# Unpacking the gate and up weights of the last feed-forward earlier, by way of a buffer in memory

## The chip, the core and the metric

The kernel runs on one core of a Trainium2 chip. The metric is the device time of one execution in microseconds (us). The engines of the core are TensorE (PE in the profile; its weight loads are PEld), VectorE (DVE), ScalarE (ACT), GpSimd (POOL) and SyncE (SP), which here only issues transfers (DMA). Each engine takes its instructions in a fixed order, and an instruction that waits holds up all that stand behind it on the same engine.

## What is computed

A decoder of two layers on 4 sequences of 512 tokens with 512 features. Each of the six steps is followed by a residual sum and a layer norm:

```python
x = _layernorm(x + _L0_attn_ref(x, ...))     # A: attention with rotary positions
x = _layernorm(x + _L0_xattn_ref(x, ...))    # B: cross attention
x = _layernorm(x + _L0_ffn_ref(x, ...))      # C: ternary weights, 8-bit activations, Hadamard
x = _layernorm(x + _L1_attn_ref(x, ...))     # D: causal attention, 16 heads
x = _layernorm(x + _L1_xattn_ref(x, ...))    # E: cross attention with a mask
x = _layernorm(x + _L1_ffn_ref(x, ...))      # F: weights packed in 4 bits
```

The change is about the weights of F. Its reference, cut down:

```python
def _dequant_fp4(packed_i32, scales_f16, group_size):
    nib = w[:, :, None] >> shifts & jnp.uint32(15)      # eight 4-bit codes in a word
    vals = _FP4_LUT[nib.astype(jnp.int32)].reshape(out_f, in_p * 8)
    return vals * s_full                                # one scale for each group of 128
w_gu = _dequant_fp4(gate_up_packed, gate_up_scales, GROUP_SIZE)
w_down = _dequant_fp4(down_packed, down_scales, GROUP_SIZE)
gate_up = jnp.einsum('bsh,oh->bso', x, w_gu)
gate, up = (gate_up[..., :I], gate_up[..., I:])         # I = 1408
h = jax.nn.silu(gate) * up
y = jnp.einsum('bsi,hi->bsh', h, w_down)
return y / jnp.sqrt(jnp.mean(y * y, axis=-1, keepdims=True) + 1e-6)
```

## The kernel before

The letters A to F above name the six steps in the kernel too, with the number of the sequence: F0 is the last feed-forward on sequence 0. `lanes` runs two of these at a time. Each is a Python generator; it records instructions up to a `yield`, then the other goes on. So the end of one step is recorded among the beginning of the next: the last of C beside D0, E3 beside F0. A `Pipe` defers a piece of work by some yields. From what is recorded a scheduler makes each engine's order, in which an instruction may stand well before or behind the place where it was recorded.

Weights are prepared by further generators, kept in `net.bg`. The list `BESIDE` says during which steps such a generator is advanced by one yield at each round; `need` runs one on until the weights that a step is about to use are there.

All tiles are 128 partitions wide and 2 KB deep. They come from pools of fixed numbers of buffers: `o` (69 buffers: weights, operands and probabilities), `t` (13, short-lived), `x` (12, rows of the residual) and `w` (4, raw weights as they are loaded). A tile can be filled when the last reader of the buffer's former tile is done. Nearly all loads and stores go through SP's one queue, in order.

F's gate and up weights are 22 tiles of 128 x 512: 11 slices of 128 hidden features, each with a gate tile (u = 0) and an up tile (u = 1); the down weights are 11 tiles. In memory a packed word stands eight times, once for each of its codes, so that a packed tile has the size of the unpacked one, 256 KB. `l1_ffn_weights` unpacks on VectorE. For gate and up there are three instructions a tile: the shifts (L1024), the mask (L1025) and the multiplication by 2^126 (L1030) that makes the code's bits a number; the scale is put on behind the matmul (`scaled`, L1064, L1067, L1070). For down weights the first two are the same, the third puts the scale on as well (L1034), and the tile is split into a high part (ScalarE, L139) and a low one (GpSimd, L142). The packed tile is loaded to a `w` buffer, worked on in place, and only the third step writes an `o` tile, `gu`. This generator, "F", is advanced beside E2, and otherwise by `need` at the head of each slice in F0. F1 to F3 find all weights unpacked.

In `l1_ffn` each slice takes 16 matmuls (L1106), one for each of the 4 groups of features, the high and the low part of x, and gate and up; then the scales, SiLU (L1078), the product (L1082), its split (L1087, L1088), and 12 matmuls for the down weights (L1097).

The end of C matters too: its 16 Hadamard results are stored to a scratch in memory (L638), loaded again in another layout (`z`), go through matmuls (L715), a maximum on VectorE (L661), a copy (L663), five small operations, a scaling on ScalarE (L681), a rounding on VectorE (L682), transposes and the down projection (L701).

Of the kernel before, what the change touches and what calls it, by code (L numbers as in the profile page):

```python
# [10 lines left out]
F32 = mybir.dt.float32  # L11
F32R = mybir.dt.float32r
F16 = mybir.dt.float16
BF16 = mybir.dt.bfloat16
I32 = mybir.dt.int32
U8 = mybir.dt.uint8
AF = mybir.ActivationFunctionType
ALU = mybir.AluOpType
# [3 lines left out]
B, S, D = 4, 512, 512  # L22
P = 128
# [9 lines left out]
D_NEXT = 7  # L33
B_NEXT = 13
F_LOAD = 5
F_SCALED, F_ACT, F_PAIR, F_DOWN = 1, 5, 3, 9
ORDER = "A0 A1 A2 A3 B0 B1 B2 B3 C0 C1 C2 C3 D0 D1 D2 D3 E0 E1 E2 E3 F0 F1 F2 F3"

BESIDE = [("A1", "A3", "C0"), ("A3", "B0", ("B", 0)), ("B0", "B2", "C"), ("C3", "D0", "D"), ("E2", "E2", "F")]


class Pipe:


    def __init__(self):
        self.todo = []
# [21 lines left out]
class Net:  # L68
    def __init__(self, ctx, tc, args):
        self.tc = tc  # L70
        self.nc = tc.nc
        self.a = args
        self.n = 0
        pool = lambda name, **kw: ctx.enter_context(tc.tile_pool(name=name, **kw))
        self.const = pool("const", bufs=1)
        self.op = pool("op", bufs=O_BUFS)
        self.tp = pool("tp", bufs=T_BUFS)
        self.xp = pool("xp", bufs=X_BUFS)
        self.wp_ = pool("wp", bufs=W_BUFS)
        self.small = pool("small", bufs=4)  # L80
        self.psum = pool("psum", bufs=8, space=PSUM)
        nc = self.nc
        tc.keep_in_program_order(nc.scalar.preload_act_table_set(LOG_EXP))
        self.ident = self.c("ident", [P, P])
        make_identity(nc, self.ident)
        self.ident16 = self.c("ident16", [P, P], BF16)
        nc.vector.tensor_copy(self.ident16, self.ident)
        self.ones = self.c("ones", [P, P])
        nc.gpsimd.memset(self.ones, 1.0)
        scratch = lambda name, shape: nc.dram_tensor(name, shape, F32, kind="Internal").ap()  # L90
        self.had_scratch = scratch("had_scratch", (2, NT, 2048, P))
        self.xd = [args["x"]] + [scratch(f"x{i}", (B, S, D)) for i in range(1, 6)] + [args["out"]]
        self.bg, self.table = {}, None
        self.gu, self.dn = {}, []
        self.pre = {}
        self.w1 = {}
        self.mean, self.scale = {}, {}
        self.tern = {name: {} for name in self.TERNARY}
# [909 lines left out]
        yield from self.value_rows(pipe, pT, cn, x, em[:, 8:12], 4, b)  # L1008


    def l1_ffn_weights(self):

        nc, a = self.nc, self.a
        pipe = Pipe()
        i4 = self.load(self.c("i4", [P, 3], I32), a["i4"])
        sh4, msk4, c6 = i4[:, 0:1], i4[:, 1:2], i4[:, 2:3]
        gs = self.load(self.c("gs16", [P, 88], F16), a["gu_s"])
        self.gs = self.c("gs", [P, 88])
        with self.tc.issue_after(self.mark.ins):
            nc.vector.tensor_copy(self.gs, gs)  # L1020

        def bits(w):

            nc.vector.tensor_scalar(w, w, sh4, c6, ALU.logical_shift_left, ALU.arith_shift_right)  # L1024
            nc.vector.tensor_scalar(w, w, msk4, None, ALU.bitwise_and)  # L1025
            return w.bitcast(F32)

        def codes(i, u, w):
            self.gu[i, u] = self.o("gu", F32R)
            nc.vector.tensor_scalar(self.gu[i, u], bits(w), 2.0 ** 126, None, ALU.mult)  # L1030

        def down(w, sc):
            f = bits(w)
            nc.vector.scalar_tensor_tensor(f, f, 2.0 ** 126, sc, ALU.mult, ALU.mult)  # L1034
            self.dn.append(self.split(f, "p4", lo_eng=nc.gpsimd))

        for i in range(11):
            for u in range(2):
                pipe.tick()
                pipe.later(F_LOAD, codes, i, u, self.load(self.w("p4", I32), a["gu_p"][i, u]))  # L1040
                yield
            pipe.tick()
            sc = self.load(self.t("p4s", F16), a["dn_s"][i : i + 1, :].to_broadcast([P, 512]))
            pipe.later(F_LOAD, down, self.load(self.w("p4", I32), a["dn_p"][i]), sc)
            yield
        yield from pipe.drain()
# [90 lines left out]
def lanes(order, task, step):  # L1137

    todo = [(e.strip("+!"), e[0] == "+", max(1, e.count("!"))) for e in order]
    plain = [name for name, _, _ in todo]
    live, done = {}, set()
    n, said = 0, 9
    while todo or live:
        if todo and len(live) < 2:
            name, soon, times = todo[0]
            before = chr(ord(name[0]) - 1) + name[1]
            if (before in done or before not in plain) and (said >= times or not live or soon):
                todo.pop(0)  # L1150
                live[name] = task(name)
                last = name
                n, said = n + 1, 0
        for name, g in list(live.items()):
            word = next(g, "end")
            if word == "end":
                live.pop(name)
                done.add(name)
            elif word == "next" and name == last:
                said += 1  # L1160
        step(n)


def body(tc, args, phases=range(6)):
    with ExitStack() as ctx:
        net = Net(ctx, tc, args)
        net.gamma = net.load(net.c("gamma", [P, 1]), args["gamma"].to_broadcast([P, 1]))
        if 0 in phases:
            net.l0_attn_weights()
        net.bg = {("B", 0): net.l0_xattn_ctx(0), "C0": net.l0_ffn_scales(), "C": net.l0_ffn_weights(), "D": net.l1_attn_weights(), "F": net.l1_ffn_weights()}  # L1170
        f = [net.l0_attn, net.l0_xattn, net.l0_ffn, net.l1_attn, net.l1_xattn, net.l1_ffn]
        plain = ORDER.replace("+", "").replace("!", "").split()
        order = ORDER.split() if len(phases) == 6 else ["ABCDEF"[p] + str(b) for p in phases for b in range(B)]

        def step(n):
            if len(phases) == 6:
                for first, last, key in BESIDE:
                    if plain.index(first) < n <= plain.index(last) + 1:
                        next(net.bg[key], None)

        def start(name):
            return f["ABCDEF".index(name[0])](int(name[1]))

        lanes(order, start, step)
# [68 lines left out]
```

## Time and profile before

| | us |
|---|---|
| median of 3 runs | 1629.89 |
| lowest and highest of them | 1626.9, 1636.79 |
| the profiled execution | 1630.29 |
| its span, from the first to the last instruction | 1628.6 |
| DMA issued by SP that carry packed gate and up words (22 of 256 KB), from issue to landing | 2.7 |

In the profile a stretch of time is given in us from the span's start. A row of busy time by stretch has the stretch, its length, then for each engine the busy time and in brackets the number of instructions, and at the end PE's granted clock, the share of the transfer engines and GB/s. A row of one line's instructions has the least, the median and the greatest duration in ns. A row of the timeline has the start, the duration, the engine, the line, the operation and the tiles (written <- read). By these rows, C3 ends near 780 us, D runs from 760 to 1160, E from 1150 to 1280, F0 from 1264 to about 1390, and F1 to F3 take 80 us each.

### The profile page before, as it was taken

To read this page: it belongs to the slowest core of one execution; us is meant where nothing else is said; L and a number is where in the kernel's file an instruction comes from. 1 tells how busy PE (TensorE), PEld (TensorE's weight loads), DVE (VectorE), ACT (ScalarE), POOL (GpSimd) and SP (SyncE) were. 2 spreads that over 40 slices of the span, in tenths; PEclk is the share of its full clock that TensorE was granted. 3 is DMA by queue.
4 is the path that set the end of the run, shared out by engine and by line. 5 is a ranking of instruction groups with operands and counts; after the bars stand their busy time and mean duration, and the time that the engine had idled before them with its cause. 6 is when DMAs were issued, how large, how long until landed. Compare 5 with 4: busy or idle time off the path is not lost.

```text
span 1628.6 us, 25543 instructions
## 1 busy us (share of the span) xinstructions
PE 1532.3 (94%) x8215; PEld 1100.0 (68%) x8246; DVE 1247.6 (77%) x2684; ACT 1010.6 (62%) x2177; POOL 665.9 (41%) x672
## 2 busy tenths in 40 slices
PE   7999999999999999899999999999998889999995
PEld 5888786444544664476777767777676766687774
DVE  6476589999875788977575766657779898979795
ACT  4333336988777887787796756967543445454542
POOL 6663563555535204422334243342333244333332
PEclk9999999999999999999999999999999999999998
DMA  7143344455124734861523334232446331111000
GB/s 241 35 149 123 110 149 137 146 172 174 59 75 132 222 116 136 250 188 61 145 60 77 79 90 117 60 86 68 155 155 196 128 113 53 43 37 52 1 26 26
DMA packets 127812, 180.76 MB, mean 111 GB/s; under 512 B 16560, under 2 KB 51376, under 8 KB 127680
## 3 DMA queue, kind: packets, MB, share of 16 engines
q1 hardware_dynamic: 123552, 170.69, 33.7%
q0 software_dynamic: 4128, 8.46, 2.1%
q8 instruction: 65, 1.06, 0.3%
q14 instruction: 67, 0.55, 0.1%
HBM read 111.98 MB, written 41.94 MB: 95 GB/s over the span
## 4 chain that ended last, share of the span: by engine, by line
PE 61%; DVE 17%; ACT 9%; issue 5%; DMA 4%; POOL 3%; SPq 1%; DVEq 0%; ACTq 0%; POOLq 0%
PE fg L1106 7%; PE facc L1097 6%; PE dT L883 3%; PE bo L458 2%; ACT de L873 2%; PE dn L701 2%; PE bT L213 2%; DVE x L200 2%; PE pu L649 2%; PE bs L486 2%; DVE bsm L434 2%; PE pg L647 2%; PE do L903 2%; DVE fg L1070 2%; PE dq L150 2%
## 5 line engine op out<-in xcount | busy, mean ns | idle before, releaser
L1070 DVE SCALAR_TENSOR_TENSOR fg<-fg,gs,fg 128x512 f32<-128x512 f32 x220 | 162.4, 745 | 35.4 <-PE fg L1106 15.2
L869 DVE CUSTOM_DVE_ANT_0 de<-ds,negm,thr 128x128 f32<-128x128 f32 (+3 forms) x256 | 126.4, 546 | 34.3 <-PE ds L858 31.2
L1106 PE MATMUL fg<-fxh,gu 128*128 128x512 f32 x352 | 143.7, 408 | 8.0 <-DVE fg L1070 5.0
L873 ACT ACTIVATE de<-de,dm 128x128 f32<-128x128 f32 (+3 forms) x256 | 143.1, 563 | 12.4 <-DVE dm L869 11.9
L1106 PE MATMUL fg<-fxl,gu 128*128 128x512 f32 x352 | 138.8, 394 | 0.0
L442 POOL TENSOR_SCALAR be<-be,bsm 128x512 f32<-128x512 f32 x128 | 95.8, 761 | 104.5 <-DVE bsm L440 72.8
L624 POOL TENSOR_TENSOR hl<-g,hh 128x512 fp32r<-128x512 f32 x64 | 83.9, 1318 | 113.3 <-ACT hh L623 98.7
L1074 POOL TENSOR_TENSOR fg<-fg,fg 128x512 f32<-128x512 f32 x44 | 61.1, 1388 | 127.1 <-ACT fg L1067 74.5
L436 ACT ACTIVATE be<-bs,bsm 128x512 f32<-128x512 f32 x128 | 87.3, 690 | 31.3 <-DVE bsm L434 29.6
L800 POOL TENSOR_TENSOR dql<-dqf,dqh 128x512 fp32r<-128x512 f32 x32 | 41.3, 1290 | 155.3 <-ACT dqh L799 121.0
L883 PE MATMUL dT<-ident,de 128*128 128x128 f32 x640 | 89.6, 278 | 7.6 <-ACT de L873 5.8
L1106 PEld LDWEIGHTS fg<-fxh,gu 128*128 128x128 f32 x352 | 66.9, 190 | 38.4 <-DVE fg L1070 14.8
L883 PEld LDWEIGHTS dT<-ident,de 128*128 128x128 f32 x640 | 71.7, 141 | 25.3 <-ACT de L873 13.6
L1064 ACT ACTIVATE fg<-fg,gs 128x512 f32<-128x512 f32 x88 | 60.4, 686 | 39.2 <-PE fg L1106 38.6
L434 DVE TENSOR_REDUCE bsm<-bs 128x1 f32<-128x512 f32 x128 | 83.3, 672 | 0.0
L1097 PE MATMUL facc<-p4h,fhh 128*128 128x512 f32 x176 | 71.2, 406 | 8.9 <-DVE fg L1070 6.2
L458 PE MATMUL bo<-bpT,cT 128*64 128x512 f32 x256 | 76.9, 618 | 2.1 <-ACT bpT L449 1.2
L213 PEld LDWEIGHTS bT<-ident,be 128*128 128x128 f32 x512 | 55.0, 141 | 34.6 <-issue 10.3
L213 PE MATMUL bT<-ident,be 128*128 128x128 f32 x512 | 73.2, 281 | 4.4 <-POOL be L442 2.1
L1067 ACT ACTIVATE fg<-fg,gs 128x512 f32<-128x512 f32 x44 | 30.3, 688 | 73.4 <-PE fg L1106 73.4
L312 POOL TENSOR_TENSOR z<-z,rope_cos 128x512 f32<-128x512 f32 x32 | 45.7, 1438 | 73.0 <-DVE zs L310 66.0
L1106 PEld LDWEIGHTS fg<-fxl,gu 128*128 128x128 f32 x352 | 66.8, 190 | 11.9
(332 smaller groups left out, 4693.3 us busy)
## 6 DMA issues: line engine op xcount, KB each, us to landing
x<-x SPq DMA_DIRECT2D x176, 256.0 KB, 3.1
had_scratch<-hw SPq DMA_DIRECT2D x64, 256.0 KB, 2.4
z<-had_scratch SPq DMA_DIRECT2D x64, 256.0 KB, 5.8
stk<-dqh SPq DMA_DIRECT2D x192, 64.0 KB, 2.0
tw<-in_wg_t SPq DMA_DIRECT2D x32, 256.0 KB, 3.8
tw<-in_wu_t SPq DMA_DIRECT2D x32, 256.0 KB, 3.6
tw<-in_wd_t SPq DMA_DIRECT2D x32, 256.0 KB, 2.9
p<-in_gu_p SPq DMA_DIRECT2D x22, 256.0 KB, 2.7
```

The costliest lines, as they stand in the source:

```text
L213: self.nc.tensor.transpose(pt[:, i * P : (i + 1) * P], srcs[i][:, j * P : (j + 1) * P], self.ident)
L434: nc.vector.tensor_reduce(sm[:, h : h + 1], ps, AX.X, ALU.max, negate=True)
L436: nc.scalar.activation(e, ps, AF.Exp, bias=sm[:, h : h + 1], accum_out=sm[:, 2 + h : 3 + h])
L442: nc.gpsimd.tensor_scalar(es[h][i], es[h][i], sm[:, 4 + h : 5 + h], 1.0, ALU.mult, ALU.mult)
L458: nc.tensor.matmul(po[0][h * 64 : h * 64 + 64, :], cT[j][:, c : c + 64], pTs[h], start=j == 0, stop=j == NT - 1)
L624: nc.gpsimd.tensor_tensor(lo, g, hi.bitcast(F32), ALU.subtract)
L869: nc.vector.tensor_tensor_reduce(es[i], ps, self.negm[:, 384 - P * i :], -1.0, self.thr[:, i : i + 1], ALU.add, ALU.min, n4[:, i : i + 1])
L873: nc.scalar.activation(es[i], es[i], AF.Exp, bias=n4[:, i : i + 1], scale=-1.0, accum_out=den[:, hh * 4 + i : hh * 4 + i + 1])
L883: nc.tensor.transpose(pt[:, o + (i - j) * P : o + (i - j + 1) * P], es[i][:, j * P : (j + 1) * P], self.ident)
L1070: nc.vector.scalar_tensor_tensor(y[u], ps, s, y[u], ALU.mult, ALU.add)
L1097: nc.tensor.matmul(acc[t], h[l][:, c], self.dn[i][r], start=i == 0 and n == 0, stop=i == 10 and n == 2)
L1106: nc.tensor.matmul(ps, self.gu[i, u][:, g * P : (g + 1) * P], xT[g][n], start=n == 0, stop=n == 1)
```

## The change

A new generator "F0" (`l1_ffn_codes`) takes over the unpacking of the gate and up tiles. It is advanced beside D1 to D3, three yields for each tile. It unpacks each to a `w` buffer and, two yields later, stores that to a new buffer in memory, `gu_codes`. `l1_ffn_weights` now loads each gate or up tile from there straight to its `o` buffer; the down weights are unpacked as before. The constants for the shifts and the mask are loaded by the new generator. (The diff's line numbers beyond L40 move by 2, and those of `l1_ffn` by 18.)

```diff
+CODES_EVERY = 3
...
-BESIDE = [("A1", "A3", "C0"), ("A3", "B0", ("B", 0)), ("B0", "B2", "C"), ("C3", "D0", "D"), ("E2", "E2", "F")]
+BESIDE = [("A1", "A3", "C0"), ("A3", "B0", ("B", 0)), ("B0", "B2", "C"), ("C3", "D0", "D"), ("D1", "D3", "F0"), ("E2", "E2", "F")]
...
+        self.gu_codes = scratch("gu_codes", (22, P, 512))
...
-    def l1_ffn_weights(self):
+    def l1_ffn_codes(self):
...
-        def codes(i, u, w):
-            self.gu[i, u] = self.o("gu", F32R)
-            nc.vector.tensor_scalar(self.gu[i, u], bits(w), 2.0 ** 126, None, ALU.mult)
+        self.bits = bits
+
+        def codes(n, w):
+            v = self.w("gu")
+            nc.vector.tensor_scalar(v, bits(w), 2.0 ** 126, None, ALU.mult)
+            pipe.later(2, lambda: nc.sync.dma_start(self.gu_codes[n], v))
+
+        for n in range(22):
+            pipe.tick()
+            pipe.later(2, codes, n, self.load(self.w("p4", I32), a["gu_p"][n // 2, n % 2]))
+            for _ in range(CODES_EVERY):
+                yield
+        yield from pipe.drain()
+
+    def l1_ffn_weights(self):
+
+        nc, a, bits = self.nc, self.a, self.bits
+        pipe = Pipe()
...
-                pipe.later(F_LOAD, codes, i, u, self.load(self.w("p4", I32), a["gu_p"][i, u]))
+                self.gu[i, u] = self.o("gu", F32R)
+                self.load(self.gu[i, u].bitcast(F32), self.gu_codes[i * 2 + u])
                 yield
...
-        net.bg = {..., "F": net.l1_ffn_weights()}
+        net.bg = {..., "F0": net.l1_ffn_codes(), "F": net.l1_ffn_weights()}
```

More of the change, by code (lines that the diff above doesn't have):

```diff
@@ L1169, in body @@
             net.l0_attn_weights()
-        net.bg = {("B", 0): net.l0_xattn_ctx(0), "C0": net.l0_ffn_scales(), "C": net.l0_ffn_weights(), "D": net.l1_attn_weights(), "F": net.l1_ffn_weights()}
+        net.bg = {("B", 0): net.l0_xattn_ctx(0), "C0": net.l0_ffn_scales(), "C": net.l0_ffn_weights(), "D": net.l1_attn_weights(), "F0": net.l1_ffn_codes(), "F": net.l1_ffn_weights()}
         f = [net.l0_attn, net.l0_xattn, net.l0_ffn, net.l1_attn, net.l1_xattn, net.l1_ffn]
```

## The prediction

> **What bounds the kernel now.** I read the page first, then the busy time by stretch, then the rows of the unpacking lines, the waits and the chain. The page says that no engine is full over the whole span:
>
> ```profile
> span 1628.6 us, 25543 instructions
> PE 1532.3 (94%) x8215; PEld 1100.0 (68%) x8246; DVE 1247.6 (77%) x2684; ACT 1010.6 (62%) x2177; POOL 665.9 (41%) x672
> ```
>
> So the stretch matters. The stretches from where the work is taken (1220 to 1380 us: the last cross attention and the first batch F0 of the last feed-forward), where it goes (690 to 780 us), and two to compare with, columns PE, PEld, DVE, ACT, POOL busy:
>
> ```profile
> 690.00:780.00 90.00, 87.54 (x608) 64.12 (x617) 68.28 (x178) 68.87 (x112) 22.63 (x29) 1.00 0.43 131
> 1160.00:1200.00 40.00, 40.00 (x198) 32.97 (x198) 33.99 (x68) 14.80 (x34) 10.72 (x10) 1.00 0.39 131
> 1220.00:1280.00 60.00, 51.54 (x247) 41.79 (x245) 55.89 (x114) 22.28 (x49) 21.61 (x17) 0.97 0.55 180
> 1280.00:1380.00 100.00, 92.36 (x382) 67.25 (x381) 94.82 (x161) 47.48 (x78) 42.16 (x30) 1.00 0.30 91
> 1380.00:1460.00 80.00, 76.57 (x337) 60.60 (x337) 67.26 (x113) 39.78 (x69) 29.37 (x22) 1.00 0.12 40
> 1460.00:1540.00 80.00, 76.91 (x332) 60.93 (x331) 65.53 (x111) 39.64 (x69) 30.66 (x23) 0.98 0.08 27
> 1500.00:1520.00 20.00, 20.00 (x89) 16.54 (x89) 15.60 (x22) 9.29 (x15) 8.07 (x7) 1.00 0.23 79
> ```
>
> DVE is nearly full from 1220 to 1380 (150.7 of 160 us). PE's busy time looks high, but its count of matmuls doesn't: 382 in 100 us beside F0, 669 in the 160 us of the next two batches, 89 in 20 us where nothing waits. From 690 to 780 DVE has 21.7 us idle, and PE is at 87.5 of 90. The unpacking itself:
>
> ```profile
> L1024 DVE TENSOR_SCALAR p<-p,i x33: 507/539/1607, 670.2 to 1359.4; 128x512 int32<-128x512 int32 x33
> L1025 DVE TENSOR_SCALAR p<-p,i x33: 450/476/1483, 675.8 to 1360.2; 128x512 int32<-128x512 int32 x33
> L1030 DVE TENSOR_SCALAR gu<-p x22: 392/416/1517, 1220.3 to 1359.9; 128x512 fp32r<-128x512 f32 x22
> 1330.24 1.48 DVE L1024 TENSOR_SCALAR p<-p,i 128x512 int32<-128x512 int32 x1
> 1331.64 0.41 DVE L1030 TENSOR_SCALAR gu<-p 128x512 fp32r<-128x512 f32 x1
> 1331.98 0.47 DVE L1025 TENSOR_SCALAR p<-p,i 128x512 int32<-128x512 int32 x1
> 1332.38 0.53 DVE L1024 TENSOR_SCALAR p<-p,i 128x512 int32<-128x512 int32 x1
> ```
>
> From start to start the three steps take 0.46, 0.40 and 0.34 us, 1.20 a tile; where POOL is working one of them can last 1.5 us.
>
> **Taken out beside F0.** 1280 to 1380 holds L1024 14.59 us, L1025 9.41 and L1030 5.39. Two thirds of the first two belong to gate and up, so DVE loses 16.0 + 5.4 = 21.4 of 94.8 us, which leaves 73.4. At the next batches' share of DVE (67.26 of 80) that needs 87.4 us. PE's 382 matmuls need 91.4 us at the next batches' pace and 85.8 us at the dense one. The gain is 8.6 to 14.2; I take 10.5, as DVE's own figure (12.6) lies between. PE is late next: in the built program its order beside F0 turns into the even pattern of the later batches.
>
> **Taken out of the cross attention.** 1220 to 1280: (7.91 + 6.01) x 2/3 + 6.17 = 15.5 us of DVE out of 55.9. At the pace of 1160 to 1200 (198 in 40 us) the 247 matmuls would need 49.9 us, so at most 10 us come free, at least none: the chain there also has a context load of 4.03 us (1224.05) and POOL's L142, which stay. I take 3.5.
>
> **Loads instead of packed words.** 22 loads take the place of 22, of the same 256 KB, 2.8 us to landing. They now wait for a buffer of the large pool on SP's queue, where before DVE's last step did. Behind the first five stand the context loads of batch 2, behind the next ten the context loads of batch 3, stores and F0's x. The tiles that held these buffers are read last by matmuls and copies of batches 0 to 2, the latest of the first fifteen by transposes of batch 1's probabilities near 1242; the store behind them went out at 1248.5. Nothing to 3 us; I take 0. The four word buffers now hold only down weights, so four L1034 and their splits move up to 1172 (three more there, 0.6 us each, in 6 idle us of DVE before 1200): 0 to 1.8, taken as 0.
>
> **Put in at 690 to 780.** The order of the built program tells what the diff doesn't: nearly all tiles are unpacked ahead of or just behind the first projections of the causal attention, within the end of layer 0's feed-forward, from the rows of 669 us on; only two tiles' steps stand near 800. 62 of the 66 instructions stand before 775. Eight such already ran there (four tiles' first two steps, for one of them down weights), so 54 are new: x 0.40 = 21.6 us into 21.7 idle ones. That idle time is mostly waiting in a chain (7.7 us for ACT's L681, 7.0 for the down projection), and every maximum, scale and rounding of that chain stands behind an inserted step. If half of it can be used, DVE slips by some 10 us; PE's matmuls follow in a fixed order, but the last steps lie behind the last split that PE needs (766). I take 7, with 0 (all of it fits; a gain has no source) and 21.6 (nothing fits) as ends.
>
> The stores wait on SP for the last step of a tile. Ahead of the 16 z loads of the last batch, which went out at 718.5, now stand the stores of the seventh and eighth tile, whose steps fall at about 715 and 720: SP's queue passes DVE's slip on to z, and so to L715. A store there takes 0.85 us of the transfers (256 KB at the 307 GB/s of 720 to 730). That is part of the 7. Later stores stand ahead of x stores and loads for batches not begun, which cost nothing, and of the first stk copies at 770, 4 us behind their own step.
>
> **Put in at 795 to 830.** Eight steps for down weights and four for gate and up, 0.43 us each: 5.2 us, where ACT is busy 19.4 of 20 us (800 to 820) and fed by DVE, which has 6.6 idle us there. I take 1, ends 0 and 5.2.
>
> **POOL's part.** Of the 33 rows of L1024, the 14 that overlap work on POOL last 1.18 us on average, the other 19 last 0.53; POOL works 36% of 1220 to 1280 and 42% of 1280 to 1380, but 0.3 us in the 10 from 710. So a step is dear where it is taken and cheap where it is put, and both sums above have it, as they use each place's rows. The Trainium skill, "SBUF — State Buffer", section "Who interferes with whom", has the reason: such an operation and GpSimd share a pair of ports, and the second to come is blocked for the whole instruction; the trace agrees. Were all steps priced at their usual 0.53, 0.47 and 0.41 us, DVE would lose 10.7 x 1.00 + 13 x 0.41 = 16.0 us beside F0 and not 21.4, need 93.7 us there, and the gain would be 6.3.
>
> **Sum.** The profiled execution took 1630.29 us, 0.4 above the median. 1630.3 - 10.5 - 3.5 + 7 + 1 = 1624.3. This is the likeliest case (chance 0.50, itself 1617 to 1631).
>
> **Rivals.** *Nothing comes of it* (0.26): other waits follow. Beside F0 the chain also passes POOL (L142 1.67 us at 1353.68, L1074 1.43 at 1356.60), and PE's waits are for ACT as much as for DVE (L1064 2.4 us against L1070 1.6). Against it, DVE is at 20.0 of 20 from 1320 to 1360. The gain would be the 8.6 alone, against 8: 1630. By the Trainium skill, "Perfetto Trace Analysis", section "Identifying the Most-Contended Engine", occupancy tells the bound for VectorE; over the whole span DVE is at 77%, and work that stays on DVE would then change nothing. The trace speaks for going by stretch.
>
> *All of it comes back* (0.14): both full stretches shrink to the dense pace and the insertion finds its holes: 14.2 + 10 - 3 = 21 less, 1609. For it: the batches after F0 run with idle DVE. Against it: the waits at the borders of batches (PE 8.72 of 10 at 720; 16.37 of 20 at 1200, with DVE at 10) have other causes.
>
> *The end of layer 0's feed-forward becomes DVE's* (0.10): DVE would need 68.3 + 21.6 = 89.9 of 90 us there, so a chain that can't use its holes stretches by up to 21.6, with 3 more for z and 3 in the causal attention; with a gain of only 8.6 + 2 this gives 1647. It decides from a slip of 14 us on, which takes a use of less than a third of the holes.
>
> That the steps don't run inside the causal attention is no rival, but part of the sum: if they did (DVE at 43 to 72% from 780 to 860), the 7 would be nearer to the 1.
>
> **Range and chances.** A measurement of this kernel tells about 1% from no change, 16 us. Below 1614: nearly all of the second rival, 0.12. Above 1646: most of the third and a little of unknown waits, 0.09. Between: 0.79. The range 1611 to 1639 holds the forecast and the first rival and about half of each other.
>
> **What would show it.** Beside F0 the first stretch should take 88 to 92 us in place of 100, with DVE near 84%; the span from 1220 to 1280 should lose 2 to 6 us. Up to 690 us nothing moves; a step of the causal attention at 860 should come 5 to 11 us later. The forecast is wrong if PE keeps 382 matmuls in 100 us with DVE at 75%, or if z goes out 10 us later.

## The result, and the profile after

The changed kernel takes 1626.19 us (median of 17 runs, 1621.29 to 1630.63), the kernel before, run beside it, 1630.46 (17 runs, 1626.9 to 1636.79). The ratio is 0.997, 95% interval 0.9958 to 0.9982: 4.9 us less, sure in its sign and far inside the 1% that the prediction counts as no change. The forecast was 6.0 us less. The profiled execution of the changed kernel took 1627.51 us. Its page begins:

```profile
span 1625.7 us, 25637 instructions
PE 1532.4 (94%) x8215; PEld 1104.3 (68%) x8246; DVE 1246.1 (77%) x2684; ACT 1010.7 (62%) x2177; POOL 665.9 (41%) x672
```

The same matmuls, the same number of instructions on DVE, the same busy time within 1.5 us: nothing was saved, work was only moved. What moved shows in the busy time by stretch (columns as in the prediction; the stretches follow the same work, not the same times):

```profile
689.30:790.30 101.00, 90.74 (x608) 65.17 (x617) 89.17 (x230) 68.92 (x111) 24.62 (x29) 0.97 0.66 206
...
1285.00:1377.00 92.00, 88.49 (x383) 69.08 (x382) 80.41 (x122) 46.49 (x76) 39.82 (x30) 1.00 0.28 90
1377.00:1457.00 80.00, 76.89 (x332) 60.85 (x331) 66.64 (x112) 38.94 (x68) 29.41 (x22) 0.98 0.13 40
```

The first row holds the same 608 matmuls as 690 to 780 did before: they now take 101 us and not 90, with DVE at 89.2 in place of 68.3. The second holds F0: 383 matmuls in 92 us where 382 took 100, with DVE at 80.4 in place of 94.8. The third, F1, is as it was.

The other way to read two traces of nearly the same program is the lag: for each matmul, its start in the one trace less its start in the other, by line, operand and rank. Median lag against the trace of before, in us, over the matmuls that start in before within 20 us of the time given (the runs e1 to e12 are the experiments below):

| | 260 | 660 | 740 | 860 | 1160 | 1240 | 1280 | 1400 |
|---|---|---|---|---|---|---|---|---|
| changed kernel | -0.3 | -2.1 | 8.2 | 11.4 | 13.1 | 8.0 | 4.2 | -2.4 |
| e1 neither | -0.1 | -1.3 | -0.8 | -0.9 | 0.8 | -4.1 | -6.6 | -13.4 |
| e2 unpacking only | -0.5 | -0.1 | 5.5 | 8.2 | 8.2 | 1.7 | -0.4 | -6.9 |
| e3 stores only | 0.5 | 0.5 | 3.5 | 3.3 | 5.0 | -0.6 | -2.8 | -9.4 |
| e5 held | -0.2 | -2.2 | -4.7 | -2.4 | 4.4 | -2.4 | -4.5 | -12.3 |
| e6 GpSimd's queue | -0.9 | -1.0 | 26.0 | 27.7 | 27.8 | 21.0 | 19.0 | 11.1 |
| e9 early | 34.0 | 32.5 | 32.0 | 31.9 | 31.5 | 24.8 | 21.1 | 12.3 |
| e12 early, large pool | 16.4 | 15.2 | 16.5 | 16.5 | 16.4 | 11.6 | 7.8 | 1.2 |

A stage costs what the lag grows by in it. Two or three us of any such number come and go between executions of one kernel (the last section has a part of the reason), so the medians of the runs decide on sums and the lag on places. For the changed kernel it says: a loss of some 12 us between 690 and 860, a gain of 8.9 beside the last cross attention (1160 to 1280) and 6.6 beside F0.

What PE waits for from 690 to 800 us (columns: what waited and for what, us in total, times, longest), first in the changed kernel, then before:

```profile
PE had L717 <- DMA z<-had_scratch: 5.5, 1, 5.5
PE dq L153 <- DVE dxl L144: 2.4, 2, 1.6
PE q2T L690 <- DVE q L684: 1.6, 3, 0.9
```

```profile
PE had L715 <- ACT q2f L663: 1.2, 1, 1.2
PE dn L701 <- ACT q2T L693: 0.7, 1, 0.7
```

One wait for z is nearly half of it. The timeline of SP's queue tells why (start, duration of the issue; x16 are the z loads of the last batch), first in the changed kernel, then before:

```profile
711.75 0.44 SPq L1035 DMA_DIRECT2D gu_codes<-gu  x1
713.83 0.37 SPq L640 DMA_DIRECT2D had_scratch<-hw  x1
715.34 0.33 SPq L219 DMA_DIRECT2D p<-in_gu_p  x1
716.02 0.37 SPq L640 DMA_DIRECT2D had_scratch<-hw  x1
716.49 0.45 SPq L1035 DMA_DIRECT2D gu_codes<-gu  x1
720.22 0.33 SPq L219 DMA_DIRECT2D p<-in_gu_p  x1
720.65 0.38 SPq L1035 DMA_DIRECT2D gu_codes<-gu  x1
721.20 12.08 SPq L219 DMA_DIRECT2D z<-had_scratch  x16
```

```profile
713.96 2.55 SPq L638 DMA_DIRECT2D had_scratch<-hw  x2
718.54 10.23 SPq L217 DMA_DIRECT2D z<-had_scratch  x16
```

z went out 2.7 us later than before, for two reasons of about the same size. The last store of what z reads went out at 716.0, about as before (716.2), but took 3.6 us to land in place of 2.3; z waits for that landing, and could have gone out at 719.6. By then the queue stood, from 716.9 to 720.2, in front of a packed load that waited for one of the four word buffers, which is freed by a store that waits for a step on DVE. The first z load then took 4.3 us to land, not 3.3. So the traffic of the change is in this wait, and not the queue's order alone.

### The profile page after: what moved, and what is told of

Its sections match the earlier page's. It is cut to its first block, busy times and chain, and to the rows that moved or that the text cites. A ratio compares the mean times of both kernels' runs of the same rounds, so it can differ in the third digit from the quotient of the medians.

```text
span 1625.7 us, 25637 instructions
## 1 busy us (share of the span) xinstructions
PE 1532.4 (94%) x8215; PEld 1104.3 (68%) x8246; DVE 1246.1 (77%) x2684; ACT 1010.7 (62%) x2177; POOL 665.9 (41%) x672
## 4 chain that ended last, share of the span: by engine, by line
PE 62%; DVE 17%; ACT 6%; issue 5%; DMA 5%; POOL 3%; SPq 1%; DVEq 0%; ACTq 0%; POOLq 0%
PE fg L1124 8%; PE facc L1115 6%; PE dT L885 3%; PE pg L649 2%; DVE bsm L436 2%; PE pu L651 2%; ACT de L875 2%; PE do L905 2%; PE had L717 2%; PE dn L703 2%; DVE fg L1088 2%; PE bo L460 2%; DVE x L202 2%; PE pv L154 2%; PE pv L153 2%
## 5 line engine op out<-in xcount | busy, mean ns | idle before, releaser
L1088 DVE SCALAR_TENSOR_TENSOR fg<-fg,gs,fg 128x512 f32<-128x512 f32 x220 | 162.9, 746 | 40.4 <-PE fg L1124 20.3
L875 ACT ACTIVATE de<-de,dm 128x128 f32<-128x128 f32 (+3 forms) x256 | 143.1, 563 | 12.2 <-DVE dm L871 11.1
```

The source lines that it names most:

```text
L875: nc.scalar.activation(es[i], es[i], AF.Exp, bias=n4[:, i : i + 1], scale=-1.0, accum_out=den[:, hh * 4 + i : hh * 4 + i + 1])
L1088: nc.vector.scalar_tensor_tensor(y[u], ps, s, y[u], ALU.mult, ALU.add)
```

## The experiments

Two theories of the cost: "queue", that it comes from what the change puts ahead of z on SP's queue, and "slip", that it comes from the steps on DVE. Then: whether another place is cheaper, and which tiles the gain comes from. Differences in us are taken from the ratio, times 1631; each ratio is against the kernel before on the same chip.

**e1, the gain alone.** No early unpacking, no stores; the 22 loads read another buffer of the same size:

```diff
-        for n in range(22):
-            pipe.tick()
...
+        yield
...
-                self.load(self.gu[i, u].bitcast(F32), self.gu_codes[i * 2 + u])
+                self.load(self.gu[i, u].bitcast(F32), self.other(i * 2 + u))
```

> Neither the early unpacking nor the stores; the last feed-forward loads 22 tiles of another scratch (the Hadamard results) as its gate and up weights, so the output is not the reference's. This is the gain alone. If the two traces are read rightly (7.8 us less from 1200 to 1285, 8.0 less from there to 1400), it takes 1630.5 - 16 = 1614 (1611 to 1618); by the prediction's 14 it is 1616. If nothing came of the relief, 1625 or more.

Measured: 1614.77 us, ratio 0.9894 (0.9876 to 0.9911), 17.3 us less (14.5 to 20.2 by the interval). That is the whole gain; so the changed kernel pays 12.4 of it back. By the lag the gain is smaller, 14.2 from 1160 to 1400.

**e2, the early unpacking alone.** The steps as in the change, the stores left out, the loads as in e1:

```diff
-            pipe.later(2, lambda: nc.sync.dma_start(self.gu_codes[n], v))
```

> The early unpacking runs on VectorE, but nothing is stored; the feed-forward loads the other scratch as in the run without both, so the output is not the reference's. Theory 'queue' (z loads stand behind stores that wait for an unpacking step): only VectorE's own slip is left, 3 to 5 us over the run without both, about 1618. Rival 'slip' (the steps themselves delay the chain): 10 to 13 over it, about 1626.

Measured: 1623.67 us, ratio 0.9943 (0.9926 to 0.996), 9.3 us less: the steps, with their loads, cost 8.0. PE's waits from 690 to 800 us:

```profile
PE had L717 <- ACT q2f L683: 2.5, 1, 2.5
PE dq L153 <- DVE dxl L144: 1.1, 2, 0.9
PE dn L703 <- ACT q2T L695: 0.9, 1, 0.9
```

PE's longest wait is down from 5.5 to 2.5 us, and yet the lag reaches 8.2 us at 860. The profile puts that wait down to ACT, but z is in it too, as SP's queue shows:

```profile
718.08 0.36 SPq L640 DMA_DIRECT2D had_scratch<-hw  x1
721.45 10.92 SPq L219 DMA_DIRECT2D z<-had_scratch  x16
```

No store of the change stands ahead of z here, and z still goes out as late as in the changed kernel: the last store of what it reads is late and takes 3.2 us to land. The first z load landed at 724.5, and PE's wait ended at 724.7. So z is late without the queue's help, PE itself having come 1.4 us behind by 700; and 2.7 us of the lag are made behind z, from 740 to 820. "Queue" falls as the only cause.

**e3, the stores alone.** 22 loads of other weights and 22 stores of them in the same places, no steps:

```diff
-            pipe.later(2, codes, n, self.load(self.w("p4", I32), a["gu_p"][n // 2, n % 2]))
+            pipe.later(4, lambda n, w: nc.sync.dma_start(self.gu_codes[n], w), n, self.load(self.w("gu"), self.other(n)))
```

> 22 loads and 22 stores at the same places, but no unpacking (the tiles come from the attention's weights and go to the buffer as they are; the output is not the reference's). 'Queue': a store waits only for its load, so z goes out within 1 us of the old time and the run takes 0 to 2 us more than the run without both, about 1616. Rival 'transfers' (11.5 MB more beside z): 6 to 10 more, about 1623.

Measured: 1617.58 us, ratio 0.9909 (0.989 to 0.9928): the traffic costs 2.4 us by the ratios, though the interval overlaps that of e1. PE waits for z here too:

```profile
PE had L717 <- DMA z<-had_scratch: 6.8, 1, 6.8
```

The lag is -3.7 ahead of that wait and 3.5 behind it, 3.0 more than at 660. No store waits for a step in this run. But the last store of what z reads, issued at 713.8, took 3.2 us to land; z went out at 718.56, 1.5 us behind that landing and behind four stores of the change; and its first load took 5.2 us to land. "Queue" is near in the number, but not in the reason that it gave.

**e4, the stores on GpSimd's queue,** all else as changed:

```diff
-            pipe.later(2, lambda: nc.sync.dma_start(self.gu_codes[n], v))
+            pipe.later(2, lambda: nc.gpsimd.dma_start(self.gu_codes[n], v))
```

> The changed kernel with its 22 stores issued by GpSimd in place of SyncE. 'Queue': z passes the stores, PE's wait of 5.5 us for z and the slow clock behind it go, 6 to 9 us less than the changed kernel, about 1618. 'Slip': no change, 1626. GpSimd then waits for the steps itself, behind which its own splits and small scales stand; if that hurts, up to 3 us more.

Measured: 1624.57 us, ratio 0.995 (0.9935 to 0.9965), 8.2 us less, between the two theories; the interval overlaps that of the changed kernel, so a gain from moving the stores alone is not shown. PE still waits for z:

```profile
PE had L717 <- DMA z<-had_scratch: 5.8, 1, 5.8
```

z went out at 720.03, behind a packed load at 719.51: that load, still on SP's queue, stands ahead of it. The last store of what z reads, issued at 715.14, had landed at 718.8.

**e5, the steps held back.** The three steps of a tile may not be placed before the DVE copy of the causal attention's transposed probabilities that was recorded last ahead of them (not a copy of its projections, as the expectation has it):

```diff
+                if n == 1:
+                    self.dmark = copied
...
+            with self.tc.issue_after(self.dmark.ins):
+                nc.vector.tensor_scalar(v, bits(w), 2.0 ** 126, None, ALU.mult)
```

> The changed kernel with the 66 unpacking steps held back on VectorE until the last copy of the causal attention's projections, so that they run between about 843 and 1051 us, inside the causal attention, and none at 690 to 780 us; loads, stores and the last feed-forward stay as in the changed kernel. Theory 'place' (the 12 us are the price of the end of layer 0's feed-forward, whose steps wait for one another, and the causal attention has room on VectorE): at most 5 us of the cost are left, 1614 to 1619 us beside 1633 of the kernel before on this chip, and the step of the causal attention at 860 comes within 2 us of where it was before. Theory 'amount' (66 steps cost VectorE the same wherever they stand): the time of the changed kernel, 1625 to 1629 us, with the lag built up by 1060 us instead of 800.

Measured: 1621.59 us, ratio 0.9947 (0.9932 to 0.9963), 8.6 us less. From 660 to 820 the lag doesn't grow, so the end of layer 0's feed-forward costs nothing any more; but from 820 to 1160 it grows by 9. Both theories fell: the place matters, and the causal attention isn't free either. Two views show why. The groups of the three steps (busy us, mean ns), first of e5, then of the changed kernel:

```profile
L1028 DVE TENSOR_SCALAR p<-p,i 128x512 int32<-128x512 int32 x26 | 19.0, 739 | 0.0
L1037 DVE TENSOR_SCALAR gu<-p 128x512 f32<-128x512 f32 x22 | 17.3, 789 | 0.9 <-DMA gu_codes<-gu 0.8
L1029 DVE TENSOR_SCALAR p<-p,i 128x512 int32<-128x512 int32 x26 | 16.1, 627 | 0.3
```

```profile
L1026 DVE TENSOR_SCALAR p<-p,i 128x512 int32<-128x512 int32 x26 | 16.6, 646 | 1.5 <-DMA p<-in_gu_p 1.5
L1027 DVE TENSOR_SCALAR p<-p,i 128x512 int32<-128x512 int32 x26 | 15.3, 594 | 0.2
L1034 DVE TENSOR_SCALAR gu<-p 128x512 f32<-128x512 f32 x22 | 10.8, 490 | 0.1
```

A tile takes 2.16 us of DVE in the causal attention and 1.73 at the end of layer 0's feed-forward, where GpSimd works less. And the stretch from 940 to 980, e5 and then before:

```profile
940.00:980.00 40.00, 34.90 (x186) 25.54 (x186) 33.97 (x59) 17.29 (x40) 18.08 (x20) 0.96 0.51 153
```

```profile
940.00:980.00 40.00, 37.39 (x211) 27.40 (x210) 24.68 (x52) 18.62 (x44) 17.10 (x20) 1.00 0.33 93
```

DVE's 15.3 us of idle time in this stretch were not room for 9.3 us of work: PE gets 186 matmuls done in place of 211. Its longest wait there, 2.6 us, is for L938 on DVE, a multiplication of the attention's outputs: at 953.97 an unpacking step of 1.49 us stands ahead of it, and it takes 1.75 us itself.

**e6, loads and stores on GpSimd's queue:**

```diff
-            pipe.later(2, lambda: nc.sync.dma_start(self.gu_codes[n], v))
+            pipe.later(2, lambda: nc.gpsimd.dma_start(self.gu_codes[n], v))
...
+            w = self.w("p4", I32)
+            nc.gpsimd.dma_start(w, a["gu_p"][n // 2, n % 2])
```

> The changed kernel with both its packed loads and its stores on GpSimd's queue, so that nothing of the change stands ahead of the z loads on SyncE's. Theory 'two prices' (VectorE's slip about 8 us, the queue ahead of z about 3 to 4): z goes out within 1 us of the last store of its operand, TensorE's wait for z is under 2.5 us, and the time is 1621 to 1624 us beside 1633 before. Theory 'z is all of it': 1616 to 1618 us. Theory 'the slip is all of it' (z would then be late for the last Hadamard results and not for the queue): 1625 to 1628 us.

Measured: 1639.58 us, ratio 1.0068 (1.0043 to 1.0094), slower than both. All three theories missed. GpSimd's timeline (in brackets the idle time before a row and what ended it):

```profile
711.72 0.76 POOL L1040 DMA_DIRECT2D p<-in_gu_p  x1 [4.26 <-issue]
712.47 0.55 POOL L1035 DMA_DIRECT2D gu_codes<-gu  x1
713.03 2.71 POOL L626 TENSOR_TENSOR hl<-g,hh 128x512 fp32r<-128x512 f32 x2
...
726.02 0.54 POOL L1040 DMA_DIRECT2D p<-in_gu_p  x1 [4.39 <-DMA gu_codes<-gu]
726.55 0.55 POOL L1035 DMA_DIRECT2D gu_codes<-gu  x1
727.13 0.31 POOL L675 TENSOR_SCALAR cm<-am,wd_t_mean 128x1 f32<-128x1 f32 x1
```

The queue that was to be freed was given another victim. GpSimd issues in order with its own work: a load that waits for a word buffer holds up `hl`, an operand of the matmuls, and `cm`, a scale that the sums of layer 0 on DVE need, and so DVE, and so the next step, and so the buffer. PE's longest wait there is 7.3 us, for such a sum (L707). The lag was 26 us at 740. What z's place in the queue costs by itself is therefore not isolated; e3 puts stores and loads at 2.4 us, and the changed kernel against e2 the stores at 4.4, both differences of runs whose intervals overlap.

**e7 and e8, the gain in two parts.** As e1 for the first 12 tiles or the last 10; the others are unpacked as before the change:

```diff
+                if i < 6:
+                    self.gu[i, u] = self.o("gu", F32R)
+                    self.load(self.gu[i, u].bitcast(F32), self.other(i * 2 + u))
+                else:
+                    pipe.later(F_LOAD, late, i, u, self.load(self.w("p4", I32), a["gu_p"][i, u]))
```

> The gain alone for the first 12 gate and up tiles, those taken beside the last cross attention: no early unpacking and no stores; these 12 are loaded as other values of the same size (rows of the scratch of the Hadamard results), so the weights of six of the eleven slices are left out of the computation; the other 10 tiles are unpacked beside F0 as before. As the prediction has it: 3.5 us from the cross attention and about 2.4 us for the two tiles whose steps fall into F0, together 6, 1627 us beside 1633 before. If the cross attention gives as much as the trace of the changed kernel suggests (7 to 8 us by 1285): 1624 to 1626 us.

> The gain alone for the last 10 gate and up tiles, those taken beside F0: no early unpacking and no stores; these 10 are loaded as other values of the same size, so the weights of five slices are left out of the computation; the first 12 are unpacked beside the cross attention as before. As the prediction has it (10.5 us for F0 less what the two tiles of the other run are worth): about 8 us, 1625 us beside 1633 before, and nothing before 1280 us. If PE is late next at once: 4 to 6 us, 1627 to 1629. If the two halves hide one another, the sum of the gains of this run and of the one with the first 12 is well under 17 us, the gain with all 22.

Measured: 1617.88 us, ratio 0.9923 (0.9903 to 0.9943), 12.6 less, for the first 12; 1624.28, ratio 0.9962 (0.9947 to 0.9977), 6.2 less, for the last 10. The sum, 18.8, is the 17.3 of e1 within the intervals: the halves don't hide one another, and two thirds of the gain hang on the tiles taken from the cross attention. The stretch that shows it, before and then e7:

```profile
1216.00:1246.00 30.00, 25.57 (x121) 20.62 (x119) 28.49 (x57) 13.29 (x28) 13.41 (x10) 1.00 0.40 123
```

```profile
1216.00:1246.00 30.00, 30.00 (x146) 24.70 (x145) 24.13 (x51) 13.47 (x29) 13.54 (x11) 1.00 0.58 185
```

Here DVE was full and PE had 121 matmuls; with the steps gone PE is dense, with 146. The timeline of DVE before shows the steps at work:

```profile
1232.57 2.13 DVE L1024 TENSOR_SCALAR p<-p,i 128x512 int32<-128x512 int32 x2
1234.62 0.87 DVE L1025 TENSOR_SCALAR p<-p,i 128x512 int32<-128x512 int32 x2
1235.41 0.41 DVE L1030 TENSOR_SCALAR gu<-p 128x512 fp32r<-128x512 f32 x1
1235.75 0.68 DVE L991 CUSTOM_DVE_ANT_0 ee<-es,pen 128x512 f32<-128x512 f32 x1
```

L991 scales the scores, adds the mask and finds the extreme of each row, and ACT's exponential, the transposes and the sums behind it wait for it; it stands behind five unpacking steps that nobody needs before F0.

**e9 and e10, much earlier.** Beside the projections of layer 0's attention, where PE was without waits and DVE had 6 to 22 us idle in 40; the diff is that of e9, and e10 has 8 for 14:

```diff
-CODES_EVERY = 3
+CODES_EVERY = 2
...
-("D1", "D3", "F0")
+("A0", "A3", "F0")
...
+        while not hasattr(self, "mark"):
+            yield
+        for _ in range(14):
+            yield
```

> The changed kernel with its 22 tiles unpacked beside the projections of layer 0's attention instead: packed loads, the 66 steps and stores all between about 55 and 225 us, two yields a tile. There TensorE has been without waits (40.00 us busy in 40 in the kernel before from 40 to 160 and from 200 to 240) and VectorE idle for 6 to 22 us in 40, but GpSimd works 16 to 27 us in 40. Theory 'place' (a step costs only where the work ahead of TensorE waits for VectorE): TensorE keeps its lead, its lag at 240 us is under 2 us, nothing moves from there to 1200 us, and the time is 1614 to 1617 us beside 1631 to 1633 of the kernel before, the whole gain. Theory 'amount' (steps that last longer beside GpSimd cost as much here as elsewhere): a lag of 5 to 10 us at 240 us and 1620 to 1625 us, as with the steps held inside the causal attention.

> The same with the first packed loads six yields sooner, from about 20 us on, where the transfers for the first projections are still under way (239 GB/s from 0 to 40 us in the kernel before), and the last steps at about 190 us. Theory 'place' with room on the queue: within 2 us of the other early version. Rival 'the start is bound by transfers': each of the first six 256 KB loads ahead of others on SyncE's queue delays TensorE there by up to 0.9 us, 2 to 5 us together, so 1616 to 1622 us, with the lag already there at 60 us.

Measured: 1643.55 us, ratio 1.0092 (1.0067 to 1.0116), and 1637.09, ratio 1.0042 (1.0023 to 1.006). Both slower than before; the theory "place" fell badly. The gain is whole (the lag falls by 19 from 1160 to 1400), but 34 us are lost by 260. In e10 the lag at 60 is -0.4: the start isn't bound by transfers, so its rival fell too. "Within 2 us" of e9 missed as well: the two lose alike up to 200 us, and 22.8 against 34.0 us by 260. PE's clock has a part in this: it is at half for 30.6 us in e9 (137 to 288 us), for 17.0 in e10, and for none in the kernel before from 40 to 500 us, which can make up to half of that time, 15 and 8 us, of the two losses. The longest of DVE's waits in e9, from 60 to 290 us:

```profile
DVE p L1030 <- DMA p<-in_gu_p: 14.1, 12, 2.2
DVE qkl L144 <- ACT qkh L141: 7.4, 5, 2.5
DVE asm L360 <- PE as L154: 7.3, 3, 4.8
```

DVE stands idle in front of a step whose packed words haven't landed (L1030 is the shift here), with the attention's own work behind it. A tile takes 2.38 us of DVE here (849, 893 and 633 ns on average). And "PE without waits" turned out to mean that PE sets the pace there: whatever delays it is lost in full.

**e11, held, first 12 tiles only,** six yields a tile; the last 10 as before the change:

```diff
-CODES_EVERY = 3
+CODES_EVERY = 6
...
-        for n in range(22):
+        for n in range(12):
```

> The version held inside the causal attention, with only the first 12 tiles unpacked early, six yields a tile in place of three (steps thinly spread from about 850 to 1110 us); the last 10 tiles are unpacked beside the last feed-forward as before the change. The run with the first 12 alone gained 12.6 us and that with the last 10 alone 6.2; held steps cost 9 us for 22 tiles. Theory 'in proportion': cost 12/22 of 9 = 5, so 7.5 us under the kernel before, 1621 to 1623 beside 1629 to 1631. Theory 'bunching' (the held steps cost where several tiles fall together, 940 to 970 us and from 1010 on): cost 1 to 2, so 10 to 12 us under, 1618 to 1620. If most of the cost comes from any step in the causal attention: 1624 or more.

Measured: 1622.65 us, ratio 0.9952 (0.9936 to 0.9968), 7.8 less: "in proportion", as far as the times go. The lag grows by 7.0 from 900 to 1160, more than that theory's 5. "Bunching" is not borne out: its 10 to 12 us less lie at the edge of the interval (5.2 to 10.4), and thinly spread steps come out no cheaper.

**e12, early, with tiles of the large pool** for the packed words, and six yields from load to step:

```diff
-            pipe.later(2, codes, n, self.load(self.w("p4", I32), a["gu_p"][n // 2, n % 2]))
+            pipe.later(6, codes, n, self.load(self.o("p4", I32), a["gu_p"][n // 2, n % 2]))
...
-            v = self.w("gu")
+            v = self.o("gu")
```

> The version unpacked beside the projections of layer 0's attention (14 us slower than before), with tiles of the large pool in place of the four word buffers, and six yields instead of two from load to step. Theory 'word buffers' (the loads of packed words and of layer 0's scales share four buffers, so that each load goes out only when VectorE has freed one, and VectorE then waits in its place for words: 14.1 us in 12 waits from 60 to 290 us): these waits fall under 3 us, the lag at 260 us falls from 34 to under 10, the time to 1615 to 1625 us. Theory 'no slack on TensorE' (the attention's own steps stand behind the unpacking on VectorE, 1.2 to 3.2 us a tile beside GpSimd): the lag stays over 20 us, 1635 to 1645 us.

Measured: 1633.21 us, ratio 1.0031 (1.0012 to 1.005); the lag at 260 is 16.4 in place of 34.0. Half of the loss went with the word buffers and the longer lead, half did not, so neither theory holds alone. (The time at half clock fell too, from 30.6 to 13.6 us.) DVE still waits for packed words, more rarely but longer:

```profile
DVE p L1030 <- DMA p<-in_gu_p: 9.5, 4, 3.4
```

That the order of DVE was at fault in the rest, and not the number of steps, was not tried.

Of the versions that leave nothing out, e5 is the quickest, 8.6 us under the kernel before; its interval (0.9932 to 0.9963) overlaps that of the changed kernel (0.9958 to 0.9982) by a little, and e4 (8.2) and e11 (7.8) are not to be told from it. e1's 17.3 us is what a place that costs nothing would give. None was found.

## Why the prediction was right in its sum, and where not

The time came 1.9 us above the forecast, but by luck: gain and cost were both taken too small and made up for one another. The gain was 17.3 and not 14.0 (by the interval 14.5 to 20.2; the lag has 14.2 to 15.5), the cost 12.4 and not 8.

*Beside F0, 10.5.* The stage took 92 us in place of 100, at the edge of the 88 to 92 named, with DVE at 87% and not 84. By the stretch that is 8, by the lag 6.6 (6.8 in e1). The step "PE is late next" fits; the size taken was too large: F0 came to the pace of the next batches, the 91.4 us of the prediction's lower end, and not to DVE's figure of 87.4. Of PE's remaining waits there, 2.1 us of 2.9 are for `fg` from DVE (L1088), within the slice.

*The last cross attention, 3.5.* This is the step that failed most: 7.4 (e1) to 8.9, outside the 2 to 6 named, within the ends of 0 to 10. "At the pace of 1160 to 1200 the 247 matmuls would need 49.9 us", a gain of 10.1, came near; the 6.6 taken off it for the context load and for GpSimd was too much. Only 1.2 to 2.7 of the 10.1 were missing. Up to 1246 PE runs dense with the steps gone (30.00 of 30 in e7), and in the changed kernel it still waits 5.2 us for the exponentials. The average over 60 us hid that the first half of them was DVE's alone (28.49 of 30).

*Loads in place of packed words, 0.* Right: PE has no wait for `gu` from 1200 to 1400 us, though the loads took 4.4 us to land, not 2.8 (the page of before has 2.7).

*Put in at 690 to 780, 7.* This is the term that was sized wrong: by the lag it is 11.0 us up to 770. The price of the steps was right, 20.9 us (89.17 less 68.28) against 21.6, and so was "if half of it can be used, DVE slips by some 10 us": DVE's idle time fell from 21.7 to 11.8 us and the stretch grew by 11.0. What failed is the sentence after that, "the last steps lie behind the last split that PE needs". PE does not catch up, and 8.9 us of lag were made between 700 and 740, before those last steps. Most of these are the wait for z, 5.5 us where before had 1.2 in the same place, with the half clock behind it (last section); 1.6 are three waits for the rounding on DVE (L684). z and its queue were named as part of the 7. But z is not the whole: in e2 and e4 too the lag grows behind 740, by 2.7 and 2.4 us up to 820, and e2, where the stores are gone, still pays 8.0. The step at 860 came 11.4 us late, just beyond the 5 to 11 named.

*Put in at 795 to 830, 1.* Within its ends: the lag grows by about 1 from 770 to 860.

*The rivals.* "Nothing comes of it" had 1630 with a gain of 8.6: e1 refutes its mechanism, though the time is near. "All of it comes back" had a gain of 24.2 against 17.3, though the cross attention did reach the dense pace in its first half, and a cost of 3 against 12.4. "The end of layer 0's feed-forward becomes DVE's" was to decide from a slip of 14 us on; the slip was 11. Its kind of loss did come where steps were put elsewhere: e6 and e9.

That the 7 would be nearer to the 1 if the steps ran inside the causal attention was wrong: e5 put them there, and they cost about 9.

## What to carry to other kernels

An engine's idle time is no room as such: at the three places tried here, 66 steps of together 38 to 52 us on VectorE cost 9 to 34 us. They stand in one order with short steps that others wait for, and they bring loads and stores that wait for buffers; how much of the cost is the one and how much the other is open. Before moving work, ask of the new place how much of a delay TensorE would pass on, and of the old one in which part of the stage the engine is really full. A transfer that can wait (for a buffer, or for a result) must not stand on a queue ahead of one that is needed soon, nor among the instructions of an engine that computes.

## What the hardware did that was not expected

PE's clock falls in steps. Between the start and the last 20 us the granted clock is at half six times in the trace of before, each time for 3.4 us; in the changed kernel for nine such periods. Two of these, one behind the other, run from 724 to 730.5 us; the first begins during the 5.5 us that PE waits for z. The stretch from 720 to 740, changed kernel and then before (the third figure from the end is PE's granted clock):

```profile
720.00:740.00 20.00, 14.23 (x85) 9.72 (x87) 12.88 (x34) 10.90 (x18) 0.80 (x2) 0.83 0.75 251
```

```profile
720.00:740.00 20.00, 18.62 (x152) 14.52 (x154) 15.53 (x42) 15.54 (x25) 0.76 (x3) 1.00 0.63 208
```

So the wait is paid for again behind it, as PE's timeline in the changed kernel shows:

```profile
725.60 2.04 PE L717 MATMUL had<-had,z 128*128 128x128 f32 x8 [5.49 <-DMA z<-had_scratch]
...
732.87 1.11 PE L717 MATMUL had<-had,z 128*128 128x128 f32 x8
```

Eight matmuls take 2.04 us right behind the wait, and 1.11 when the two periods are over. A period costs up to 1.7 us, half its length. The Trainium skill, "TensorE: Matmul & The Clock Gate", section "Part 1: The HAM clock gate", has a free-running window of about 3.4 us, with half the clock behind an idle one; the 3.4 us periods agree. The traces add that most of the periods stand behind shorter waits, of 1.2 to 3.4 us, and that the same place may have one or not: before has one at 678 and one at 1470, e5 neither. e5's trace has three, and its execution of 1617.01 us is well under the median of 1621.59. Single traces of this kernel are to be compared with that in mind.

In three runs the price of the same three steps (mean durations, which overlap a little from start to start) rose with GpSimd's share of the stretch: 1.67 us a tile at 690 to 790 us (GpSimd busy 24%), 2.16 in the causal attention (36%, e5), 2.38 beside the projections of layer 0's attention (49% of 60 to 290 us, e9). A fourth doesn't fit: e12, in the same place as e9 with GpSimd busy 51%, took 1.93. The Trainium skill, "SBUF — State Buffer", section "Who interferes with whom", has the two engines share a pair of ports, and the first three points agree in direction; by the fourth the share alone doesn't set the price.
